# Q projection of layer 0: Strassen's seven products for the last four token tiles, with three tiles in both column halves during the loads

## Chip, cores and metric

The kernel runs on one core of one Trainium2 chip. The metric is the device time of one execution in microseconds (us), the median of several runs. PE is TensorE (matmuls), PEld its weight loads, DVE is VectorE, ACT is ScalarE, POOL is GpSimd and SP is SyncE, which here only issues DMAs.

## What is computed

The program is two layers on 1024 tokens (4 images of 16 x 16) with 1024 channels, all in float32. Layer 0 is the part that the change touches:

```python
x = x + L0(_gn(x))                         # group norm over 32 groups
q = _bn(einsum('bhwc,cd->bhwd', x, Wq))    # 1024 x 1024 times 1024 x 1024
k = softmax(einsum('bhwc,cd->bhwd', x, Wk))  # 256 columns
v = _bn(einsum('bhwc,cd->bhwd', x, Wv))      # 256 columns
# then a content part k.v.q and a part over relative positions, both linear in q
```

Layer 1 is causal attention with 16 heads and a mixture of 8 experts. It follows layer 0 and is the larger part of the time.

## The kernel before

**Q of layer 0.** The normalised input lies in `xn` as 8 chunks of 128 channels by 1024 tokens, the weight in two tiles `w_q[0]` and `w_q[1]`, one for each half (512) of its columns. The output has 8 token tiles `t` times 2 column halves `kc`, 16 products of 128 x 512. Each is a sum over the 8 chunks, so 128 matmuls (`q_product`, L294-295).

**Early products.** The input comes in chunk by chunk (L214-216: `xn` and `w_q[0]` of a chunk; `w_q[1]` as one load behind them, L217). While chunks arrive, six products grow together, tiles 0 to 5 of column half 0, in six PSUM banks (`early`, L310). Between their matmuls lie the group norm of the next chunk: `group_means`, `group_spreads`, `group_norm`, on DVE, ACT and PE. This loop is in an order written by hand (`manual_schedule`, L316). At its end DVE takes the reciprocal of `var_q` and makes scale and shift of the batch norm (L337, `batch_norms`).

**The other products.** The ten remaining products then run one after the other, each in a bank of the ring `mm` (3 banks; a second ring is `tr`, also 3). Outside of the hand-written stretches a scheduler sets the order on each engine.

**Leaving PSUM.** `q_out` (L297) takes a product out. One DVE multiplication (L299) by `q_scale` reads PSUM and frees the bank. Four DVE additions of `q_shift` (L303), each 64 partitions x 256 columns, then write the four quarters into `q0`, with a step of 64 bytes between columns. The scaled rows `q_s` have three buffers.

**What follows.** `w_kv` takes the buffer of `w_q[0]` (L348), so its two loads wait for the last use of `w_q[0]`. Eight products `pk` (L357) follow in the `mm` ring; each leaves through a maximum on DVE (`k_top`, L365) and an exponential on ACT (`k_e`, L368), so the fourth `pk` needs the first one's bank back. Then come the position products `pT` (L414), which read `q0` and the windows that POOL copies (L412). POOL also issues the load of `b_proj` (L496) into the buffer of `w_q[1]`.

**Strassen elsewhere.** The v projection of layer 0 and the products of layer 1 already go by seven products in place of eight, with the sums made on DVE (`sums_of_A`, L149).

Of the kernel before, what the change touches and what calls it, by code (L numbers as in the profile page):

```python
# [32 lines left out]
F32 = mybir.dt.float32  # L33
# [6 lines left out]
P = 128  # L40
C = 1024
NC = C // P
# [3 lines left out]
NT = TOK // P  # L46
# [9 lines left out]
HALF = 512  # L56
# [11 lines left out]
def kernel(  # L68
# [27 lines left out]
    nc = tc.nc  # L96

    def pool(stack, name, bufs=1, **kw):
        return stack.enter_context(tc.tile_pool(name=name, bufs=bufs, reuse_waits="tile", **kw))
# [10 lines left out]
    def big_tile(n, name, shape=(NC, TOK)):  # L110
        return big[n].tile([P, *shape], F32, tag="big", name=name)

    def w_tile(name, *parts, home=None, queue=nc.sync):

        w = (home or wpool).tile([P, NC, HALF], F32, tag="w", name=name)
        at = 0
        for part in parts:
            n = part.shape[1]
            queue.dma_start(w[:, :, at : at + n], part.rearrange("(c p) n -> p c n", p=P))
            at += n  # L120
        return w

    def mm(name):
        return ps.tile([P, HALF], F32, tag="mm", name=name)

    def tr(name):
        return ps.tile([P, HALF], F32, tag="tr", name=name)
# [82 lines left out]
    with ExitStack() as layer0:  # L210
        l0 = pool(layer0, "l0")
        xn = x_pool.tile([P, NC, TOK], F32, tag="x", name="xn")
        w_q = [wpool.tile([P, NC, HALF], F32, tag="w", name=f"w_q{kc}") for kc in range(2)]
        for c in range(NC):  # L214
            nc.sync.dma_start(xn[:, c, :], xT[ts(c, P), :])
            nc.sync.dma_start(w_q[0][:, c, :], Wq[ts(c, P), :HALF])
        nc.sync.dma_start(w_q[1], Wq[:, HALF:].rearrange("(c p) n -> p c n", p=P))  # L217

        vp = l0.tile([P, 4, 2], F32, tag="vp", name="vp")
        for i, a in enumerate((v_gamma, v_beta, v_mean, v_var)):  # L220
# [6 lines left out]
        with ExitStack() as projection:  # L227
            proj, projw = pool(projection, "proj"), pool(projection, "projw", 2)
# [17 lines left out]
            def group_means(c):  # L246
                stats = small.tile([P, B, 6], F32, tag="gn_stats", name=f"gn_stats{c}")
                mv = small.tile([P, B, 2], F32, tag="gn_mv", name=f"gn_mv{c}")
                for b in range(B):
                    nc.vector.bn_stats(stats[:, b, :], xn[:, c, ts(b, M)])  # L250
                    nc.vector.bn_aggr(mv[:, b, :], stats[:, b, :])
                pm = tr(f"gn_pm{c}")
                nc.tensor.matmul(pm[:, :B], average, mv[:, :, 0], start=True, stop=True)
                chunks[c] = mv, pm

            def group_spreads(c):
                mv, pm = chunks[c]
                mean = small.tile([P, B], F32, tag="gn_mean", name=f"gn_mean{c}")
                nc.vector.tensor_copy(mean, pm[:, :B])
                spread = small.tile([P, B], F32, tag="gn_spread", name=f"gn_spread{c}")  # L260
                nc.vector.tensor_sub(spread, mv[:, :, 0], mean)
                nc.vector.tensor_mul(spread, spread, spread)
                nc.vector.tensor_add(spread, spread, mv[:, :, 1])
                pv = tr(f"gn_pv{c}")
                nc.tensor.matmul(pv[:, :B], average, spread, start=True, stop=True)
                chunks[c] = mean, pv

            def group_norm(c):
                mean, pv = chunks[c]
                rstd = small.tile([P, B], F32, tag="gn_rstd", name=f"gn_rstd{c}")  # L270
                inverse_root(rstd, pv[:, :B], EPS)
                less = small.tile([P, B], F32, tag="gn_less", name=f"gn_less{c}")
                nc.vector.scalar_tensor_tensor(less, mean, -1.0, rstd, ALU.mult, ALU.mult)
                for b in range(B):
                    nc.scalar.activation(
                        xn[:, c, ts(b, M)],
                        xn[:, c, ts(b, M)],
                        AF.Identity,
                        bias=less[:, b : b + 1],
                        scale=rstd[:, b : b + 1],  # L280
                    )
# [12 lines left out]
            def q_product(pq, kc, t, c):  # L294
                nc.tensor.matmul(pq, xn[:, c, ts(t, P)], w_q[kc][:, c, :], start=(c == 0), stop=(c == NC - 1))  # L295

            def q_out(pq, kc, t):  # L297
                q_s = projw.tile([P, HALF], F32, tag="q_s", name=f"q_s{kc}_{t}", bufs=3)
                nc.vector.tensor_mul(q_s, pq, q_scale[:, ts(kc, HALF)])  # L299
                for hl in range(2):  # L300
                    rows = slice(hl * 64, hl * 64 + 64)
                    for kl in range(2):
                        nc.vector.tensor_add(  # L303
                            q0[kl * 64 : kl * 64 + 64, kc, :, :, 2 * t + hl].rearrange("p i j -> p (i j)"),
                            q_s[rows, ts(kl, M)],
                            q_shift[rows, kc * HALF + kl * M : kc * HALF + (kl + 1) * M],
                        )

            two = ps.tile([P, 2, HALF], F32, tag="sc", name="pq_two", bufs=1)
            early = [mm(f"pq0_{t}") for t in range(3)] + [two[:, 0, :], two[:, 1, :], tr("pq0_5")]  # L310

            def keep_warm(n):
                for _ in range(n):
                    nc.tensor.matmul(early[0][:, :P], average, average, start=True, stop=True)

            with tc.manual_schedule():  # L316
                keep_warm(14)
                group_means(0)
                keep_warm(3)
                group_spreads(0)  # L320
                keep_warm(5)
                group_norm(0)
                for c in range(NC):
                    for t, pq in enumerate(early):
                        q_product(pq, 0, t, c)
                        if t == 1 and c + 1 < NC:
                            group_means(c + 1)
                        elif t == (3 if c == 0 else 2) and c + 1 < NC:
                            group_spreads(c + 1)
                            group_norm(c + 1)  # L330
                    if c == NC - 4:
                        nc.vector.tensor_scalar(var_q, var_q, BN_EPS, None, ALU.add)
                        nc.scalar.activation(var_q, var_q, AF.Sqrt)
                    elif NC - 4 < c < NC - 1:
                        n = c - (NC - 3)
                        nc.vector.reciprocal(var_q[:, ts(n, M)], var_q[:, ts(n, M)])
                nc.vector.reciprocal(var_q[:, HALF:], var_q[:, HALF:])  # L337
                batch_norms()
            for t, pq in enumerate(early):
                q_out(pq, 0, t)  # L340
            for kc in range(2):
                for t in range(NT):
                    if kc or t >= len(early):
                        pq = mm(f"pq{kc}_{t}")
                        for c in range(NC):
                            q_product(pq, kc, t, c)
                        q_out(pq, kc, t)
            w_kv = w_tile("w_kv", Wk, Wv)  # L348


# [1 line left out]
            for t in range(NT):  # L352
                b, kc = divmod(t, 2)
                pk = mm(f"pk{t}")
                for c in range(NC):
                    for kl in range(2):
# [4 lines left out]
                            start=(c == 0),  # L361
                            stop=(c == NC - 1),
# [33 lines left out]
        for R, first, n_i, T in (  # L396
# [6 lines left out]
            parts = rows * SIDE  # L403
            group = 2 if n_i > S2 else 4
            for n0 in range(0, SIDE, group):
                pT = mm(f"pT{R}_{n0}")
                out_T = pT[:parts, : group * BH * n_i].rearrange("p (j i h) -> p j i h", j=group, h=BH)
                for g in range(group):
# [4 lines left out]
                    for kc in range(2):  # L413
# [4 lines left out]
                            start=(kc == 0),  # L418
                            stop=(kc == 1),
# [3 lines left out]
            for i in range(n_i):  # L423
                ni = first + i
                start = S2 * R + ni - SIDE + 1
# [10 lines left out]
        a11, a12, a21, a22 = (w_kv[:, 4 * j : 4 * j + 4, M + i * P : M + (i + 1) * P] for i in range(2) for j in range(2))  # L436
        b11, b12, b21, b22 = (xn[:, 4 * j : 4 * j + 4, ts(l, HALF)] for j in range(2) for l in range(2))
        c11, c12, c21, c22 = (v_T[:, i, ts(l, HALF)] for i in range(2) for l in range(2))
        s_w = tpool.tile([P, 3, NC // 2, P], F32, tag="s_w", name="s_w", bufs=1)
        s1, s2, s4 = (s_w[:, i, :, :] for i in range(3))  # L440
# [44 lines left out]
        for b, nt in tiles:  # L485
            t = 2 * b + nt
# [10 lines left out]
        with tc.manual_schedule(engines={mybir.EngineType.SP, mybir.EngineType.DVE}):  # L497
            for i, (b, nt) in enumerate(tiles):
# [4 lines left out]
                t = 2 * b + nt  # L503
                for hp in range(2):
                    py = mm(f"py{t}_{hp}")
                    for hl in range(2):
                        bh = b * HEADS0 + 2 * hp + hl
                        for mh in range(2):
# [4 lines left out]
                                start=(mh == 0),  # L513
                                stop=(mh == 1),
# [16 lines left out]
    with ExitStack() as attention:  # L531
# [19 lines left out]
        b11, b12, b21, b22 = (ln1[:, 4 * j : 4 * j + 4, ts(l, HALF)] for j in range(2) for l in range(2))  # L551
# [358 lines left out]
    with ExitStack() as gating:  # L910
# [304 lines left out]
        pairs = ExitStack()  # L1215
        w_odd, two = pool(pairs, "w_odd", 2, side="right"), pool(pairs, "two", 2, side="right")
# [300 lines left out]
```

## Time and profile before

| | |
|---|---|
| median of 3 runs | 1252.16 us (1251.64 to 1252.25) |
| the profiled execution: time, span | 1251.44 us, 1249.6 us |
| granted TensorE clock | 0.998 |
| PE busy | 1231.7 us (99%) |
| DVE busy | 725.6 us (58%) |
| ACT busy | 219.0 us (18%) |
| POOL busy | 359.8 us (29%) |
| DMA moved | 169.21 MB, mean 135 GB/s |
| DMA in the first of 40 slices | 350 GB/s |
| early products and group norm | until 56.4 us of the span |
| the other ten Q products | 57.49 to 126.35 us |
| the eight `pk` products | 126.35 to 154.19 us |

The span goes from the first to the last instruction of the program in one profiled execution; the time of that execution lies 1.8 us above its span. Starts in the timelines are counted from the start of the span. A float32 matmul of the program appears as two matmul records, so that 128 columns by 512 of one chunk are two records.

### The profile page before, as it was taken

How to read it: one execution, taken by the hardware profiler on the slowest of the kernel's cores; microseconds unless marked ns; L12 is line 12 of the kernel's file. 1: busy time of each engine (PE TensorE's matmuls, PEld its weight loads, DVE VectorE, ACT ScalarE, POOL GpSimd, SP SyncE). 2: the span in 40 equal slices, each digit the busy share in tenths (PEclk: the TensorE clock that was granted, in tenths of full speed). 3: DMA queues.
4: the chain of work that ended last, by engine and by line, in shares of the span. 5: the costliest groups of instructions: out<-in, count | busy, mean ns of one | idle time of the engine just before them, and what ended most of it. 6: DMA issues, size and time to landing. Idle time of an engine off the chain costs nothing.

```text
span 1249.6 us, 12749 instructions
## 1 busy us (share of the span) xinstructions
PE 1231.7 (99%) x4556; PEld 643.2 (51%) x4556; DVE 725.6 (58%) x1322; ACT 219.0 (18%) x511; POOL 359.8 (29%) x439
## 2 busy tenths in 40 slices
PE   9999999999999999999999999999999999999998
PEld 5444896777884444444444444444344434434443
DVE  5784325578422566657554866765756646565642
ACT  3300111221000222222221422110110111111110
POOL 0000052241000222232231114445552635363520
PEclk9999999999999999999999999999999999999999
DMA  9020013852202434353383557374856475656442
GB/s 350 18 68 1 17 49 88 320 200 87 68 1 68 124 112 151 118 165 114 102 276 122 187 204 271 71 223 95 245 125 179 105 232 152 153 127 194 100 82 54
DMA packets 91383, 169.21 MB, mean 135 GB/s; under 512 B 9232, under 2 KB 46112, under 8 KB 91312
## 3 DMA queue, kind: packets, MB, share of 16 engines
q1 hardware_dynamic: 73952, 115.83, 27.9%
q0 software_dynamic: 15136, 47.78, 16.0%
q10 hardware_dynamic: 2224, 4.72, 1.1%
q8 instruction: 38, 0.62, 0.2%
q14 instruction: 33, 0.27, 0.1%
HBM read 115.59 MB, written 48.50 MB: 131 GB/s over the span
## 4 chain that ended last, share of the span: by engine, by line
PE 73%; DVE 3%; ACT 1%; issue 1%; DVEq 0%; ACTq 0%
PE p L1284 31%; PE pqk L566 16%; PE po L748 7%; PE pv L566 7%; PE left L1326 3%; PE sc L661 2%; PE pa L730 2%; PE rest L1340 2%; PE last_pe L1442 1%; PE dense_pe L868 1%; PE parts L1006 0%; ACT L132 0%; DVE row_T L177 0%; DVE xb L750 0%; DVE T L1227 0%
## 5 line engine op out<-in xcount | busy, mean ns | idle before, releaser
L853 POOL DMA_INDIRECT w_e_xg<-rows,gather x146 | 155.1, 1062 | 57.3 <-issue 40.2
L1284 PE MATMUL p<-w_e,A 128*128 128x512 f32 x368 | 163.2, 593 | 1.3 <-DVE slot L1119 1.3
L703 POOL TENSOR_TENSOR s_q<-s_q,total 128x128 f32<-128x128 f32 (+1 forms) x128 | 66.2, 547 | 300.3 <-DVE total L700 297.9
L748 PE MATMUL po<-w_p,y_T 128*128 128x512 f32 x256 | 118.5, 605 | 0.0
L1284 PEld LDWEIGHTS p<-w_e,A 128*128 128x128 f32 x368 | 69.6, 190 | 89.9 <-issue 89.2
L1284 PE MATMUL p<-T,S 128*128 128x512 f32 x256 | 112.8, 593 | 0.0
L876 POOL DMA_INDIRECT out_dram<-y,add x32 | 57.0, 1781 | 176.5 <-ACT y L1290 120.2
L1290 ACT ACTIVATE y<-y,slot 128x512 f32<-128x512 f32 x64 | 46.1, 721 | 335.0 <-DVE y L1298 177.1
L295 PE MATMUL pq<-w_q,xn 128*128 128x512 f32 x224 | 99.6, 596 | 1.4 <-DVE q_s L299 1.1
L689 ACT ACTIVATE s_q<-s,top 128x256 f32<-128x256 f32 (+1 forms) x128 | 56.6, 443 | 186.1 <-issue 146.7
L566 PE MATMUL pqk<-ln,w_qk 128*128 128x512 f32 x192 | 85.6, 595 | 0.0
L1284 PEld LDWEIGHTS p<-T,S 128*128 128x128 f32 x256 | 48.5, 190 | 61.1 <-issue 60.3
L748 PEld LDWEIGHTS po<-w_p,y_T 128*128 128x128 f32 x256 | 45.9, 190 | 47.9 <-issue 46.9
L177 DVE STREAM_TRANSPOSE A<-w_e_xg 128x1024 f32<-128x1024 f32 x32 | 39.6, 1239 | 49.9 <-DMA w_e_xg<-rows,gather 49.8
L295 PEld LDWEIGHTS pq<-w_q,xn 128*128 128x128 f32 x224 | 41.8, 190 | 51.8 <-issue 47.4
L566 PE MATMUL pqk<-T,S_qk 128*128 128x512 f32 x128 | 58.5, 600 | 0.0
L566 PEld LDWEIGHTS pqk<-ln,w_qk 128*128 128x128 f32 x192 | 36.0, 190 | 43.3 <-issue 42.3
L1284 PE MATMUL p<-T,A 128*128 128x512 f32 x128 | 57.5, 592 | 0.0
L1284 PE MATMUL p<-w_e,S 128*128 128x512 f32 x128 | 57.5, 592 | 0.0
L566 PE MATMUL pv<-w_v,ln 128*128 128x256 f32 x192 | 44.3, 381 | 1.4 <-DVE ln L177 0.9
L1326 PE MATMUL left<-w_e,one 128*32 128x512 f32 x312 | 41.8, 593 | 0.0
L414 PE MATMUL pT<-q,window 128*128 128x256 f32 (+3 forms) x256 | 40.4, 320 | 0.0
(296 smaller groups left out, 1760.9 us busy)
## 6 DMA issues: line engine op xcount, KB each, us to landing
w_e<-in_expert_w_dram SPq DMA_DIRECT2D x14, 2048.0 KB, 12.9
s_rows<-s_q SPq DMA_DIRECT2D x32, 384.0 KB, 2.6
s_rows<-s_rows SPq DMA_DIRECT2D x128, 96.0 KB, 2.3
w_qk<-in_W_attnT_dram SPq DMA_DIRECT2D x8, 1024.0 KB, 6.0
xn<-in_xT_dram SPq DMA_DIRECT2D x8, 512.0 KB, 8.0
x_at<-in_x_dram SPq DMA_DIRECT2D x8, 512.0 KB, 7.6
w_v<-in_W_attnT_dram SPq DMA_DIRECT2D x2, 2048.0 KB, 12.4
x_rows<-x_at POOLq DMA_DIRECT2D x8, 512.0 KB, 3.9
```

Of the source, the lines that this page charges most:

```text
L177: nc.vector.transpose(row_T[:, :, :slots].rearrange("p c (g j) -> p g c j", j=32), row[:, : slots // 32, :].rearrange("p g (c i) -> p g c ...
L295: nc.tensor.matmul(pq, xn[:, c, ts(t, P)], w_q[kc][:, c, :], start=(c == 0), stop=(c == NC - 1))
L414: nc.tensor.matmul(out_T[:, g, :, :], window[:, kc, :, :].rearrange("p i j -> p (i j)"), q0[:, kc, first : first + n_i, nj, :], start=(kc ...
L566: nc.tensor.matmul(bank, stationary(c), moving(c), start=(c == 0), stop=(c == NC // 2 - 1))
L689: nc.scalar.activation(blocks(h, qt), s[:, h, cols].rearrange("p (b f i) -> p b f i", f=Q, i=32), AF.Exp, bias=top[:, qt, h : h + 1], accu ...
L703: nc.gpsimd.tensor_mul(blocks(h, qt), blocks(h, qt), total[:, qt, h : h + 1].unsqueeze(2).unsqueeze(3).to_broadcast([P, 1 + qt, Q, 32]),)
L748: nc.tensor.matmul(po, y_T[:, c, ts(t, P)], w_p[j][:, c, :], start=(c == 0), stop=(c == NC - 1))
L853: nc.gpsimd.indirect_dma_start(out=row[:, g, :], out_offset=None, in_=table[: (TOK - P) * Q, :] if e in SHORT else table, in_offset=bass.I ...
L876: nc.gpsimd.indirect_dma_start(out=out[: TOK - P, :] if e in SHORT else out, out_offset=bass.IndirectOffsetOnAxis(ap=add[:slots, e, k : k ...
L1284: nc.tensor.matmul(bank, a[:, c, :], b[:, c, :], start=(c == 0), stop=(c == NC // 2 - 1))
L1290: nc.scalar.mul(y[i][:, ts(j, HALF)], y[i][:, ts(j, HALF)], slot[:, e, 1, 2 * pair + i : 2 * pair + i + 1])
L1326: nc.tensor.matmul(bank[ts(i, 32), :], stationary, w[of][j][:, c, :], start=(c == 0), stop=(c == NC - 1))
```

## The change

The loads of `w_q[1]` now come chunk by chunk beside those of `w_q[0]`. The six early products are tiles 0 to 2 of both column halves, in place of tiles 0 to 5 of half 0. Tile 3 follows plainly in both halves. Tiles 4 and 5 form one pair, tiles 6 and 7 another: each pair is a 2 x 2 block product (two token tiles by two halves of the channels, times two halves of the channels by two column halves), done in seven products of 4 matmuls each. The sums of the left side go to `q_parts`, a tile in a buffer that was free at this time; those of the right side are made in place in `w_q`, once for both pairs. The results are added up in `q_parts` and scaled there in place. Of the four additions of each `q_out`, the two that stay on their partitions now run on POOL.

```diff
-            nc.sync.dma_start(w_q[0][:, c, :], Wq[ts(c, P), :HALF])
-        nc.sync.dma_start(w_q[1], Wq[:, HALF:].rearrange("(c p) n -> p c n", p=P))
+            for kc in range(2):
+                nc.sync.dma_start(w_q[kc][:, c, :], Wq[ts(c, P), ts(kc, HALF)])
...
-            def q_out(pq, kc, t):
-                q_s = projw.tile([P, HALF], F32, tag="q_s", name=f"q_s{kc}_{t}", bufs=3)
+            def q_out(pq, kc, t, q_s=None):
+                if q_s is None:
+                    q_s = projw.tile([P, HALF], F32, tag="q_s", name=f"q_s{kc}_{t}", bufs=3)
                 nc.vector.tensor_mul(q_s, pq, q_scale[:, ts(kc, HALF)])
                 for hl in range(2):
                     rows = slice(hl * 64, hl * 64 + 64)
                     for kl in range(2):
-                        nc.vector.tensor_add(
+                        (nc.gpsimd if kl == hl else nc.vector).tensor_add(
...
-            early = [mm(f"pq0_{t}") for t in range(3)] + [two[:, 0, :], two[:, 1, :], tr("pq0_5")]
+            early = [mm(f"pq0_{t}") for t in range(3)] + [two[:, 0, :], two[:, 1, :], tr("pq1_2")]
...
-                        q_product(pq, 0, t, c)
+                        q_product(pq, t // 3, t % 3, c)
...
+            parts = big_tile(0, "q_parts").rearrange("p a b -> p (a b)")
+            b11, b12, b21, b22 = (w_q[l][:, 4 * j : 4 * j + 4, :] for j in range(2) for l in range(2))
+            pairs = []
+            for pair in range(2):
+                a = [xn[:, 4 * j : 4 * j + 4, ts(4 + 2 * pair + i, P)] for i in range(2) for j in range(2)]
+                homes = [parts[:, ts(8 * pair + i, HALF)] for i in range(8)]
...
+                nc.vector.tensor_add(s1, a[2], a[3])
+                nc.vector.tensor_sub(s2, s1, a[0])
+                nc.vector.tensor_sub(s4, a[1], s2)
+                nc.vector.tensor_sub(s3, a[2], a[0])
+            for n in (1, 2, 3, 5, 4, 7, 6):
+                for pair, ((a11, a12, a21, a22), (c11, c12, c21, c22), (s1, s2, s3, s4)) in enumerate(pairs):
+                    a, b = {
+                        1: (a11, b11),
+                        2: (a12, b21),
+                        3: (s4, b22),
+                        5: (s1, b11),
+                        4: (a22, b21),
+                        7: (s3, b12),
+                        6: (s2, b22),
+                    }[n]
+                    bank = (mm if n % 2 else tr)(f"pq_pair{pair}_{n}")
+                    for c in range(NC // 2):
+                        nc.tensor.matmul(bank, a[:, c, :], b[:, c, :], start=(c == 0), stop=(c == NC // 2 - 1))
+                    if n == 1:
+                        nc.scalar.copy(c22, bank)
+                        nc.scalar.copy(c21, bank)
+                    elif n == 2:
+                        nc.vector.tensor_add(c11, bank, c22)
+                        q_out(c11, 0, 4 + 2 * pair, c11)
+                    elif n == 3:
+                        nc.vector.tensor_add(c12, bank, c22)
+                    for to in {5: (c12, c22), 4: (c21,), 7: (c21, c22), 6: (c12, c21, c22)}.get(n, ()):
+                        nc.vector.tensor_add(to, bank, to)
+                    if n == 6:
+                        q_out(c12, 1, 4 + 2 * pair, c12)
+                        q_out(c21, 0, 5 + 2 * pair, c21)
+                        q_out(c22, 1, 5 + 2 * pair, c22)
+                if n == 1:
+                    nc.vector.tensor_sub(b11, b12, b11)
+                    nc.vector.tensor_sub(b12, b12, b22)
+                elif n == 3:
+                    nc.vector.tensor_sub(b22, b22, b11)
+                    nc.vector.tensor_sub(b21, b21, b22)
```

In the built program the order of instructions differs from before only up to the softmax of `pk`; behind it both programs have the same order on every engine.

## The prediction

> **What bounds the kernel now.** First the page, part 1 and the chain of waits by engine.
>
> ```profile
> PE 1231.7 (99%) x4556; PEld 643.2 (51%) x4556; DVE 725.6 (58%) x1322; ACT 219.0 (18%) x511; POOL 359.8 (29%) x439
> ...
> PE 73%; DVE 3%; ACT 1%; issue 1%; DVEq 0%; ACTq 0%
> ```
>
> PE is busy for 99% of the span and makes up the chain, so a matmul less is time less, as long as PE doesn't wait instead. Next the stretches: busy time by engine in the ten plain Q products, then in the `pk` products.
>
> ```profile
> 57.50:126.30 68.80, 68.80 (x160) 30.30 (x160) 45.81 (x80) 1.49 (x2) 0.00 (x0) 1.00 0.10 31
> 126.30:154.20 27.90, 27.90 (x258) 25.52 (x257) 9.66 (x26) 3.96 (x14) 1.97 (x5) 1.00 0.05 19
> ```
>
> After the stretch and its length come PE, PEld, DVE, ACT, POOL. PE has no gap; DVE has 23 us to spare in the first stretch, POOL did nothing. Third, the timeline of PE where the early products end.
>
> ```profile
> 55.34 1.02 PE L295 MATMUL pq<-w_q,xn 128*128 128x512 f32 x2
> 57.49 68.93 PE L295 MATMUL pq<-w_q,xn 128*128 128x512 f32 x160 [1.12 <-DVE q_s L299]
> 126.35 27.91 PE L357 MATMUL pk<-w_kv,xn 128*64 128x256 f32 x256
> ```
>
> Here PE waits 1.12 us for DVE to free the first bank. Last, what POOL and DVE do to each other when both read two SBUF operands, since the change sets 32 POOL additions beside DVE's. Two timelines, of DVE and POOL alone:
>
> ```profile
> 284.34 2.92 POOL L526 TENSOR_TENSOR x_at<-x_at,ln_rows 128x1024 f32<-128x1024 f32 x1 [4.62 <-ACT ln_rows L196]
> 284.97 3.37 DVE L153 TENSOR_TENSOR w_v<-w_v 128x1024 f32<-128x1024 f32 x1
> ...
> 288.26 1.21 DVE L152 TENSOR_TENSOR s_v<-w_v,s_v 128x1024 f32<-128x1024 f32 x1
> ```
>
> ```profile
> 582.65 0.66 DVE L150 TENSOR_TENSOR S_qk<-w_qk 128x512 f32<-128x512 f32 x1
> 582.81 3.60 POOL L703 TENSOR_TENSOR s_q<-s_q,total 128x128 f32<-128x128 f32 x4 [3.38 <-DVE total L700]
> 583.35 0.77 DVE L151 TENSOR_TENSOR S_qk<-S_qk,w_qk 128x512 f32<-128x512 f32 x1
> 584.15 0.98 DVE L152 TENSOR_TENSOR S_qk<-w_qk,S_qk 128x512 f32<-128x512 f32 x1
> 585.06 0.88 DVE L153 TENSOR_TENSOR w_qk<-w_qk 128x512 f32<-128x512 f32 x1
> 585.86 0.68 DVE L650 TENSOR_TENSOR U_qk<-pqk,qk 128x512 f32<-128x512 f32 x1
> ```
>
> The DVE sum beside a POOL addition takes 3.37 us, its like alone 1.21. In the second view four sums start 0.80 us apart where 0.64 is usual (402.37 to 404.30), and the four POOL instructions take 3.60 us where the same four take 1.90 at 531.05. Each side waits for the other in turn.
>
> The Trainium skill (SBUF — State Buffer, Who interferes with whom) has this as a rule: a DVE instruction with two SBUF inputs and a GpSimd instruction that reads SBUF exclude each other for the whole instruction. The first view agrees (3.37 against 1.21 us); the second shows less per instruction.
>
> **Fewer matmuls.** Before, 16 products of 8. After, 8 products of 8 (tiles 0 to 3) and 2 x 7 of 4: 120, not 128. One costs 68.9/80 = 0.861 us, so PE loses 8 x 0.861 = **6.9 us**.
>
> **The 1.12 us gap.** In the built order three matmuls of product 2 (pair 0, in a `tr` bank) stand ahead of tile 3: 2.6 us of work from 56.4 to 58.9. The first `q_s` comes later, as two sums of 0.6 us stand before it on DVE: it ended at 57.43, now at 58.6. The gap goes: **1.1 us**. PE would so reach `pk` at 126.35 - 8.0 = 118.3.
>
> **Loads.** Each chunk now brings 1.05 MB, at 350 GB/s in 3.0 us; PE takes 5.75 us for one (the starts 15.15, 20.89, 26.64). Chunk 0 of `xn` is still first. SP's seven added issues stand ahead of the batch-norm rows and `emb`, with the same bytes before them. Nothing.
>
> **DVE in the chunk loop.** Two sums (1.2 us) move into chunk 4, where DVE waited 1.57 us for PE (29.54). Hidden, with 0.4 us over.
>
> **ACT.** Four copies of 0.59 us, where it idled for 70 us. Hidden.
>
> **w_kv.** Its issue on SP now waits for product 4, which ends 4 x 3.45 = 13.8 us ahead of `pk`; the K part lands 5.5 us after issue (DMA issues). Nothing queues behind it on SP until the position stage. Hidden; without that cover it would cost up to 5.5.
>
> **b_proj.** POOL's issue of it waits for the last product, with eight POOL additions behind it. `pT` needs them, some 30 us later. Hidden.
>
> **q_s.** A scaling on DVE now also waits until POOL has read the buffer three `q_out`s back, with all of DVE's queue behind it. POOL's two additions take some 1.2 us per `q_out` (0.61 for 256 columns, L703), DVE's share 1.8. Hidden, while POOL stays under 0.9 per addition.
>
> **DVE up to the right-hand sums.** From 54.35 to the last addition of tile 3 DVE has, alone: two sums 1.2, three rows of 1024 3.5, eight `q_s` 4.9, sixteen additions 9.6, four sums 2.4, small ones 0.6: until 76.6. The first in-place sum waits for product 1 of both pairs, at 79.6: 3.0 us of slack. Then until product 3 ends (90.7) it has 2 x 2.2 + 5 x 0.61 + 4 x 0.60 = 9.9 us, until 89.6: 1.1 of slack. From there 0.6 + 2 x 2.2 = 5.0 makes b21 ready at 95.8, due for product 4 at 97.6: 1.8. In all 5.9 us of slack for 20 POOL additions.
>
> **DVE's tail: the new wait.** Product 6 of pair 0 ends at 118.3 - 3.45 = 114.9. Before the first `k_top` DVE has six additions from PSUM (0.61), six scalings in place (0.61) and ten column additions (0.60): 13.3 us, until 128.3. `k_top` to the end of `k_e` takes 1.0 (130.13 to 131.15), a hand-over 0.1: the first bank is free at 129.4. The fourth `pk` wants it at 118.3 + 3 x 3.49 = 128.8. So PE waits **0.6 us** even without POOL.
>
> **POOL in the tail.** Ten POOL additions fall into this stretch, each beside a DVE instruction with two SBUF inputs. The price of one is bounded below by 0 (POOL's 2.36 us at 247.42 left the PSUM additions beside it at 0.67), above by 0.54 (the 2.15 us that L153 lost, for a quarter of the columns). In the second view a 256-column POOL instruction cost some 0.4, a 128-column one 0.2. I take 0.30: DVE's column additions hold fewer columns than those sums, so part of POOL's work fits between. Ten cost **3.0 us**. Upstream 20 x 0.30 = 6.0 against 5.9 of slack: nothing. Above that price I count half of what exceeds the slack, since many early additions find DVE waiting or reading PSUM.
>
> **The sum.** -6.9 - 1.1 + 0.6 + 3.0 = -4.4. Behind `pk` both programs have the same order, and PE fills 1177.6 of the 1191.5 us of the stretches tabled from 57.5 on, so it stays: 1251.4 goes to 1247.0 in the profiled execution; that lies 0.7 below the median, which goes to **1247.8 us**. With a price of 0 it is -7.4; with 0.54 it is -8.0 + 0.6 + 5.4 + (10.8 - 5.9)/2 = +0.5.
>
> **Rivals.**
>
> *POOL's additions mostly miss DVE's.* For it: six of the 22 DVE instructions in the tail read PSUM and collide with nothing. Against: the other 16 read SBUF twice, and each pair of POOL additions is released by a scaling right among them. At 0 to 0.15 each the gain is 7.4 to 5.9: 1244.8 to 1246.3.
>
> *The collisions eat the gain.* DVE waits out the whole of POOL's instruction each time, as L153 did. At 0.39 each the tail takes 4.5 and the stretch before it (7.8 - 5.9)/2 = 1.0, which leaves a gain of 2.5, 1249.7; at 0.60 it is 6.6 and 3.0, and 1.6 slower, 1253.8. Against: the mean of the second view.
>
> This is what the Trainium skill's rule of exclusion would give if taken in full: at 0.54, 1252.6 us.
>
> *POOL's strided addition is slow, and the kernel slower.* No POOL instruction of the trace writes columns 64 bytes apart. DVE pays for it: 0.586 us (L303) against 0.42 for 256 plain columns (L600). If POOL needs twice its plain rate, an addition holds 1.08 us in place of 0.54 and the price rises to 0.84: tail 0.6 + 8.4, before it (16.8 - 5.9)/2 = 5.4; 14.4 - 8.0 = 6.4 slower, 1258.6. It decides from a price of 0.64 on: 7.0 + 3.5 = 10.5, that is 2.5 slower. Against: POOL's plain rate, 2.36 us for 1024 columns (L526) or 2.3 ns each, is no faster than DVE's strided one, 0.586 for 256 with its fixed part, so the step may be hidden.
>
> The Trainium skill (GPSIMD Engine Reference, Performance pitfalls for Q7 kernels) puts half as much again on reads with a step over 8 bytes; here the write has the step, and no run here shows POOL's price. With it a collision would cost 0.57, and the time would be about 1253 us, short of the point that decides.
>
> *It doesn't do what it says:* `w_kv` or a chunk late, so that PE waits for a load. The slack is 8 us for the one and 2.7 per chunk for the other.
>
> **Numbers.** Chances: forecast (price 0.15 to 0.39) 0.47, its own range 1246.3 to 1249.7; collisions light 0.23; gain eaten 0.16; strided POOL slow 0.12; a load late 0.02. A measurement of this kernel can tell about 0.2%, 2.5 us. Faster: 0.47 + 0.23 = 0.70; same 0.16; slower 0.14. The range goes from the light end to the end of the eaten case, and leaves out the slow one.
>
> **What would show it.** In the trace after: 240 records of Q products rather than 256; no wait for `q_s` behind the early ones; `pk` without a wait for `w_kv`; a wait of some 3.6 us on the fourth `pk`, released by `k_e`; DVE's additions near 0.9 apart where POOL works. Wrong would be: a POOL addition over 0.9 us when alone, waits on products 4 or 5, or none at the fourth `pk`.

## The result, and the profile after

| | before | after |
|---|---|---|
| median (13 runs each) | 1251.91 us (1251.45 to 1252.43) | 1248.97 us (1248.41 to 1249.39) |
| ratio, with 95% interval | | 0.9977 [0.9968, 0.9985] |
| profiled execution: time, span | 1251.44, 1249.6 us | 1249.13, 1247.3 us |

The change saves 2.9 us, or 0.23%. 1247.8 was forecast. The page of the changed kernel, part 1:

```profile
PE 1227.9 (98%) x4540; PEld 641.3 (51%) x4540; DVE 740.8 (59%) x1322; ACT 221.1 (18%) x515; POOL 390.4 (31%) x471
```

Sixteen PE records are gone (4556 to 4540, two for each of the 8 matmuls), ACT has 4 instructions more and POOL 32, as the diff says. But PE is busy for only 3.8 us less, where eight matmuls are 6.9. Some of the remaining ones must have become longer. The timeline of PE shows where; the first two lines are the early products' end, the others the last Strassen products and `pk`. Columns are start, time, engine, line, operation, then the idle time before it and who ended it.

```profile
55.13 1.02 PE L295 MATMUL pq<-w_q,xn 128*128 128x512 f32 x2
55.99 2.74 PE L376 MATMUL pq_pair<-w_q,xn 128*128 128x512 f32 x6
...
104.31 13.90 PE L376 MATMUL pq_pair<-w_q,q_parts 128*128 128x512 f32 x32
118.14 10.64 PE L407 MATMUL pk<-w_kv,xn 128*64 128x256 f32 x96
132.62 19.17 PE L407 MATMUL pk<-w_kv,xn 128*64 128x256 f32 x160 [3.84 <-ACT k_e L418]
151.71 2.84 PE L496 MATMUL pv<-xn,w_kv 128*128 128x512 f32 x6
```

Before, tile 6 started behind a wait of 1.12 us. Here three matmuls of product 2 stand in that place and nothing waits. `pk` starts at 118.14 rather than 126.35, which is 8.2 us earlier. Then two things give time back. The fourth `pk` waits 3.84 us for the first one's exponential, and the 160 records behind this wait take 19.17 us where the first 96 set a pitch that gives 17.7. So `pv`, the next stage, starts 2.48 us earlier (154.19 before), not 8.2.

The stretch view says why the 160 records are long. After a stretch and its length come busy time (and instructions) of PE, PEld, DVE, ACT and POOL, then the granted TensorE clock (1.00 is full speed), the DMA share and GB/s:

```profile
118.14:151.71 33.57, 29.73 (x257) 25.44 (x256) 21.38 (x40) 3.96 (x14) 11.97 (x17) 0.95 0.04 17
132.60:136.10 3.50, 3.48 (x18) 2.00 (x20) 2.86 (x8) 1.00 (x4) 2.37 (x5) 0.51 0.00 0
136.10:139.60 3.50, 3.50 (x36) 3.19 (x34) 1.37 (x5) 0.70 (x4) 0.00 (x0) 1.00 0.02 5
```

For 3.413 us behind the wait PE runs at half the clock: 18 records in 3.50 us, then 36 in the next 3.50. Half of 3.413 is 1.7 us, lost on top of the wait.

What makes the wait is DVE's tail. Its timeline:

```profile
117.93 3.78 DVE L304 TENSOR_TENSOR q<-q_parts,q_rows 64x256 f32<-64x256 f32 x4
...
123.05 1.57 DVE L304 TENSOR_TENSOR q<-q_parts,q_rows 64x256 f32<-64x256 f32 x2
...
127.15 3.77 DVE L304 TENSOR_TENSOR q<-q_parts,q_rows 64x256 f32<-64x256 f32 x4
130.94 0.69 DVE L300 TENSOR_TENSOR q_parts<-q_parts,q_rows 128x512 f32<-128x512 f32 x1
131.55 0.42 DVE L415 TENSOR_REDUCE k_top<-pk 128x1 f32<-128x256 f32 x1
```

`k_top`, which starts the release of the first `pk` bank, stands behind all of them, though the first `pk` was complete near 121.7 (a third of the 96 records). Four additions beside POOL's take 3.78 us, 0.94 each. The same additions without POOL are in an experiment below.

### The profile page after: what moved, and what is told of

Read it like the earlier page. It is cut to its first block, busy times and chain, and to the rows that moved or that the text cites. A ratio compares the mean times of both kernels' runs of the same rounds, so it can differ in the third digit from the quotient of the medians.

```text
span 1247.3 us, 12776 instructions
## 1 busy us (share of the span) xinstructions
PE 1227.9 (98%) x4540; PEld 641.3 (51%) x4540; DVE 740.8 (59%) x1322; ACT 221.1 (18%) x515; POOL 390.4 (31%) x471
## 4 chain that ended last, share of the span: by engine, by line
PE 74%; DVE 2%; ACT 1%; issue 0%; DVEq 0%; ACTq 0%
PE p L1334 31%; PE pqk L616 16%; PE pv L616 7%; PE po L798 7%; PE left L1376 3%; PE sc L711 2%; PE pa L780 2%; PE rest L1390 2%; PE last_pe L1492 1%; PE dense_pe L918 1%; PE parts L1056 0%; ACT L132 0%; DVE row_T L177 0%; DVE xb L800 0%; DVE T L1277 0%
## 5 line engine op out<-in xcount | busy, mean ns | idle before, releaser
L903 POOL DMA_INDIRECT w_e_xg<-rows,gather x146 | 157.7, 1080 | 57.3 <-issue 40.8
L295 PE MATMUL pq<-w_q,xn 128*128 128x512 f32 x96 | 44.5, 599 | 0.3 <-ACT xn L275 0.3
L616 PEld LDWEIGHTS pv<-w_v,ln 128*128 128x128 f32 x192 | 37.3, 196 | 6.4 <-ACT v L639 1.2
```

What stands on the lines that cost most here:

```text
L616: nc.tensor.matmul(bank, stationary(c), moving(c), start=(c == 0), stop=(c == NC // 2 - 1))
L903: nc.gpsimd.indirect_dma_start(out=row[:, g, :], out_offset=None, in_=table[: (TOK - P) * Q, :] if e in SHORT else table, in_offset=bass.I ...
```

## The experiments

Theory: up to `pk` the change gives 8 us, and what is lost is the wait on the fourth `pk`, which DVE's tail and POOL's collisions in it make, together with the half clock that follows the wait. Rivals: the loss lies elsewhere (the loads, POOL's work over all of the stage), or the half clock is chance.

Experiments 1, 3, 4 and 5 ran in one session, in which the kernel before stood at 1253.73 us (9 runs, 1252.59 to 1256.58), 1.8 us above its time in the table and more widely spread. The changed kernel was not run in it. So neither the ratios of these experiments nor their medians beside 1248.97 are good to better than some 2 us, and their traces count for more; experiment 6 compares on one chip.

**1. All additions on DVE.** The changed kernel without POOL's share.

```diff
-                        (nc.gpsimd if kl == hl else nc.vector).tensor_add(
+                        nc.vector.tensor_add(
```

> The changed kernel with all four additions of each q_out on DVE, as before the change. Theory (moving two of four to POOL shortens DVE's queue by more than the collisions give back): the tail has ten more additions of 0.6 us in place of ten collisions of 0.34, so the fourth pk waits 3.84 + 2.6 = 6.4 us; ahead of product 4 there are 20 x 0.6 = 12 us more against 5.9 us of slack, 6 us of waits; with one or two half clocks 1256 to 1260 us, slower than before. Rival (the collisions cost as much as the move saves): about 1249.

Measured: 1259.49 us (1257.56 to 1260.29), ratio 1.0041 [1.0028, 1.0055]: slower than before. Timeline of PE:

```profile
77.69 7.99 PE L376 MATMUL pq_pair<-w_q,xn 128*128 128x512 f32 x18 [2.02 <-DVE q_s L300]
...
102.98 8.83 PE L376 MATMUL pq_pair<-w_q,xn 128*128 128x512 f32 x16 [3.57 <-DVE w_q L397]
...
136.04 2.84 PE L496 MATMUL pv<-xn,w_kv 128*128 128x512 f32 x6
142.48 13.84 PE L407 MATMUL pk<-w_kv,xn 128*64 128x256 f32 x100 [3.59 <-ACT k_e L418]
```

DVE alone is too slow: PE waits for a scaled row, for the right-hand sum b21 (L397), and at the fourth `pk` for 6.4 us, of which 2.84 are filled by matmuls of `pv`, which the scheduler put there in this version. Half clock follows the second and the third wait, for one and for two windows:

```profile
103.86:107.26 3.40, 3.40 (x5) 1.35 (x4) 1.46 (x3) 0.00 (x0) 0.00 (x0) 0.50 0.00 0
141.40:148.22 6.82, 5.74 (x28) 3.24 (x30) 4.88 (x14) 1.70 (x6) 0.00 (x0) 0.50 0.00 0
```

POOL's share, with all its collisions, is what makes the seven products pay.

**2. The loads alone, and POOL's share alone.** The kernel before with chunk-wise `w_q[1]` and three tiles in both halves, and the kernel before with two of four additions on POOL; no Strassen in either.

```diff
-            nc.sync.dma_start(w_q[0][:, c, :], Wq[ts(c, P), :HALF])
-        nc.sync.dma_start(w_q[1], Wq[:, HALF:].rearrange("(c p) n -> p c n", p=P))
+            for kc in range(2):
+                nc.sync.dma_start(w_q[kc][:, c, :], Wq[ts(c, P), ts(kc, HALF)])
...
-                        q_product(pq, 0, t, c)
+                        q_product(pq, t // 3, t % 3, c)
...
```

The edit for POOL's share is the line with `nc.gpsimd` in the change.

> The kernel before with only the loads of the change (w_q of both halves by chunk) and its six early products (tiles 0 to 2 in both halves); the ten others run plainly, without Strassen, all additions on DVE. Theory (loads and early products are hidden and worth nothing by themselves): the same chunk pitch of 5.75 us, the 1.1 us wait for the first q_s stays, 1251.9 us within 0.5. Rival (the larger chunks arrive late, or the var_q rows do): waits in the chunk loop, up to 3 us slower.

> The kernel before with only the move of two of the four additions of each q_out to POOL. Theory (DVE is not what PE waits for in the plain Q stage): no change, 1251.9 us within 0.5; DVE's column additions 0.6 us where POOL is done, 0.9 where it works. Rival (the share on POOL is a gain or a loss by itself): 1 us or more either way.

Measured, beside 1252.57 us (21 runs) of before: 1251.27 us (1250.70 to 1252.33), ratio 0.9989 [0.9980, 0.9998] for the loads; 1252.43 us (1251.94 to 1252.81), ratio 0.9997 [0.9988, 1.0006] for POOL's share. Neither moves the time by more than 0.2%. Each lies at most 0.2 us outside its expected band, which was set from the 1251.9 of before; here before stood 0.7 higher. Both keep the wait for the first `q_s`; here in the timeline of the loads alone:

```profile
57.14 3.27 PE L295 MATMUL pq<-w_q,xn 128*128 128x512 f32 x7 [1.13 <-DVE q_s L299]
...
126.00 27.91 PE L357 MATMUL pk<-w_kv,xn 128*64 128x256 f32 x256
```

The 0.35 us by which `pk` starts earlier than before are there at the last early product (54.99 against 55.34). So the loads are hidden, and the 1.1 us come from the matmuls of product 2 that stand in the gap, not from the other order of tiles. Before Strassen DVE had room, so that POOL's help is worth nothing there and its collisions cost nothing.

**3. POOL's tail additions later.** The twelve POOL additions of the last three `q_out` of both pairs are held until the third softmax step. DVE's order stays.

```diff
+                        if kl == hl and hold:
+                            held.append(operands)
+                        else:
+                            (nc.gpsimd if kl == hl else nc.vector).tensor_add(*operands)
...
+                if t == 2:
+                    gate = small.tile([P, 1], F32, tag="gate", name="gate", bufs=1)
+                    opened = nc.gpsimd.tensor_copy(gate, total)
+                    with tc.issue_after(opened.ins):
+                        for operands in held:
+                            nc.gpsimd.tensor_add(*operands)
```

> The changed kernel with POOL's twelve additions of the last six q_outs held back, by a small copy on POOL that reads a result of the third softmax step; DVE's order is unchanged. Theory (DVE's tail is longer by 3.0 to 3.4 us because POOL's additions shut it out of SBUF, ten times 0.3): DVE's column additions in the tail are 0.6 us apart, the fourth pk waits 0.6 us, no half clock; 1249.0 - 3.2 - 1.7 = 1244.1 us. Rival (DVE's column additions are slow by themselves, or the queue is simply too long): they stay near 0.94 us apart, the wait stays near 3.8 us, 1249.0.

Measured: 1245.59 us (1245.40 to 1246.99), ratio 0.9937 [0.9924, 0.9951]. The timelines of DVE, PE and POOL:

```profile
117.67 2.38 DVE L314 TENSOR_TENSOR q<-q_parts,q_rows 64x256 f32<-64x256 f32 x4
...
128.14 0.42 DVE L421 TENSOR_REDUCE k_top<-pk 128x1 f32<-128x256 f32 x1
```

```profile
129.21 17.55 PE L413 MATMUL pk<-w_kv,xn 128*64 128x256 f32 x160 [0.69 <-ACT k_e L424]
```

```profile
132.79 9.60 POOL L432 TENSOR_TENSOR q<-q_parts,q_rows 64x256 f32<-64x256 f32 x12
```

Without POOL the four additions take 2.38 us, 0.60 each, in place of 0.94. From the start of `pk` to the first `k_top` it is 128.14 - 117.88 = 10.26 us; with POOL it is 131.55 - 118.14 = 13.41. The ten POOL additions thus cost DVE 3.15 us, **0.31 each**. The wait falls to 0.69 us, no half clock follows it, and the 160 records take 17.55 us. POOL's strided addition takes 0.80 us here. `pv` starts 5.0 us earlier than in the changed kernel (146.69 against 151.71), near the 4.9 expected (3.2 + 1.7). The median misses its forecast of 1244.1 by 1.5 us: the session may account for some of it, and the profiled execution has a half clock from 277.48 on, behind another wait.

**4. The wait kept, PE busy in it.** Twelve matmuls of 128 x 128 that nothing reads stand ahead of the fourth `pk`.

```diff
+                if t == 3:
+                    fill = tr("fill")
+                    for _ in range(12):
+                        nc.tensor.matmul(fill[:, :P], average, average, start=True, stop=True)
                 pk = mm(f"pk{t}")
```

> The changed kernel with twelve matmuls of 128 x 128 that nobody reads, in a free bank, ahead of the fourth pk: 3.3 us of work inside its wait of 3.8. Theory (the half clock of 3.4 us after that wait comes from the wait): the clock stays at 1.0 in the pk stretch, the fourth pk starts at the same time, and 1.7 us go: 1247.3 us. Rival (the half clock has another cause): it stays, 1249.0; if the filler takes longer than the wait, above that.

Measured: 1247.61 us (1246.72 to 1249.75), ratio 0.9951 [0.9937, 0.9964]. Timeline of PE:

```profile
128.57 2.94 PE L407 MATMUL fill<-average 128*128 128x128 f32 x24
132.50 17.55 PE L411 MATMUL pk<-w_kv,xn 128*64 128x256 f32 x160 [0.99 <-ACT k_e L422]
149.98 2.84 PE L500 MATMUL pv<-xn,w_kv 128*128 128x512 f32 x6
```

The stretch behind the wait, which was at 0.51 in the changed kernel:

```profile
132.60:136.10 3.50, 3.50 (x34) 3.24 (x36) 2.75 (x8) 1.11 (x4) 2.26 (x5) 1.00 0.03 5
```

The fourth `pk` starts as late as in the changed kernel (132.50 against 132.62), since DVE is no faster. Yet `pv` starts 1.73 us earlier (149.98 against 151.71): useless work in the wait keeps the clock whole. This separates the two parts of the loss, 3.84 us of waiting and 1.7 us of half clock. The median is 1.4 us under the changed kernel's, but from another session. The profiled execution itself, 1249.75 us, is the slowest of the five: 3.3 us of its lead over the kernel before go between 760 and 909 us, far behind the change, with one half-clock window from 769.69 on; what took the rest is open.

**5. The last four `q_out` later.** DVE issues each of them behind the softmax step of one of the first four `pk`, so that `k_top` no longer stands behind them.

```diff
-                        q_out(c12, 1, 4 + 2 * pair, c12)
-                        q_out(c21, 0, 5 + 2 * pair, c21)
-                        q_out(c22, 1, 5 + 2 * pair, c22)
+                        late += [(c12, 1, 4 + 2 * pair), (c21, 0, 5 + 2 * pair), (c22, 1, 5 + 2 * pair)]
+                        while pair == 0 and len(late) > 1:
+                            of, kc, t = late.pop(0)
+                            q_out(of, kc, t, of)
...
-                nc.vector.tensor_scalar(k_q[:, b, kc, :], k_e, total, None, ALU.mult)
+                k_done = nc.vector.tensor_scalar(k_q[:, b, kc, :], k_e, total, None, ALU.mult)
+                if late:
+                    of, to_kc, to_t = late.pop(0)
+                    with tc.issue_after(k_done.ins):
+                        q_out(of, to_kc, to_t, of)
```

> The changed kernel with its last four q_outs (of the two pairs) issued one by one behind the softmax steps of the first four pk, so that DVE's maximum of the first pk is not behind them. Theory (PE's wait on the fourth pk comes from DVE's queue in front of the first k_top, and the half clock behind it from that wait): no wait at the fourth pk, granted clock 1.0 in the whole pk stretch, 3.8 + 1.7 = 5.5 us less than the changed kernel, 1243.5 us. Rival (the bank comes late for another reason, such as the load of w_kv or the exponential): the wait stays near 3.8 us and the time at 1249.0.

Measured: 1244.48 us (1242.77 to 1244.93), 1.0 above the forecast, ratio 0.9922 [0.9908, 0.9936]. Timeline of PE:

```profile
118.44 27.91 PE L408 MATMUL pk<-w_kv,xn 128*64 128x256 f32 x256
146.28 2.84 PE L501 MATMUL pv<-xn,w_kv 128*128 128x512 f32 x6
```

All 256 records run through in 27.91 us, as before the change, and `pv` starts 7.91 us earlier. POOL's and DVE's additions still collide here; what is late no longer matters, since `q0` is complete by 139 and first read by `pT` behind `pv`.

**6. Both once more on one chip.** The changed kernel and the version of experiment 5, unchanged, side by side, for a direct comparison and for profiles in which the clock's windows lie otherwise.

> The changed kernel once more, unchanged, for a second profile with other edges of the 3.413 us windows. If a window in which PE idles for half its length or more is followed by one at half clock, the 3.84 us wait at the fourth pk brings one at any offset (at least 1.9 us of it fall into one window), so pv starts about 2.5 us earlier than before, not 4.2; the 1.85 us wait near 279 us brings one only if nearly all of it falls into one window. Time 1248.4 to 1249.4. If the half clock of the first profile was chance, no 0.5 follows the wait here, and pv starts 4.2 us earlier, time near 1247.2.

> The last four q_out behind the softmax steps, beside the changed kernel on the same chip. If the wait at the fourth pk and its half clock are all that was lost, this is 4 to 5 us under the changed kernel: 1243.5 to 1245 against 1248.4 to 1249.4. If the gain of the first run came from its chip, the two are within 2 us.

Measured: the changed kernel 1249.09 us (11 runs, 1248.57 to 1249.78), ratio to before (1251.64, 15 runs) 0.9980 [0.9971, 0.9989]; the later `q_out` 1243.38 us (1242.39 to 1244.02), ratio 0.9935 [0.9921, 0.9948], 0.1 us under its expected band. On the same chip the rearranged version is 5.7 us faster than the changed kernel and 8.3 us faster than the one before: it is the best of all. Stretches of the changed kernel's second profile:

```profile
128.39:132.25 3.86, 0.00 (x1) 0.00 (x0) 3.79 (x6) 0.56 (x2) 2.52 (x4) 0.91 0.00 0
132.30:138.30 6.00, 6.00 (x29) 3.30 (x31) 3.31 (x10) 1.13 (x4) 2.31 (x5) 0.50 0.00 0
138.40:141.80 3.40, 3.40 (x36) 3.08 (x34) 0.94 (x3) 0.57 (x2) 0.00 (x0) 1.00 0.03 5
```

The same wait, 3.86 us, and again half clock behind it, this time for two windows: the clock goes down at 131.56, inside the wait, and up 6.83 us later. So it is no chance, but its length depends on where the windows lie: the wait now costs 3.9 and about 2.9 more (the 160 records take 20.50 us), and `pv` starts 1.5 us earlier than before, not the 2.5 expected (0.57 us of the 1.5 were there at the last early product, 54.77 against 55.34). In the first of the two windows PE still idled for 0.69 us (131.56 to 132.25), and in the first of the two of experiment 1 for 1.08 (141.40 to 142.48). The other seven falls to half clock in the ten profiles, the one at each program's end left out, lasted one window, and PE worked throughout that window.

## Why the prediction was right, and where its sum was off

The direction and the mechanism were right: matmuls gone, then a new wait of DVE's making at the fourth `pk`. The gain of 4.4 us in the profiled execution came out as 2.3 (1251.44 to 1249.13), and the medians differ by 2.9. The median of 1248.97 lies in the forecast's own range, 1246.3 to 1249.7, though a cost of more than 2 us in the profile was not in the sum: the range was made for the price of a collision and had room for it, which is luck.

- **Fewer matmuls and the gap: -8.0 forecast, -8.21 measured** at the start of `pk`, of which 0.21 were there at the last early product (55.13 against 55.34). No wait for `q_s` behind the early products; three matmuls of product 2 lie there, as worked out.
- **Loads, ACT, `w_kv`, `b_proj`, the `q_s` ring: nothing, as forecast.** No wait of PE names a load or one of ACT's copies, DVE has no wait for POOL in this stage, and the loads alone leave the time within 0.2%.
- **Slack up to the right-hand sums: held, by a hair.** 6.0 us of collisions were set against 5.9 of slack. That it held by so little is in part luck. The last sum, in DVE's timeline of the changed kernel, ends at 97.28:

```profile
94.99 2.29 DVE L397 TENSOR_TENSOR w_q<-w_q,w_q 128x2048 f32<-128x2048 f32 x1
97.20 2.48 DVE L386 TENSOR_TENSOR q_parts<-pq_pair,q_parts 128x512 f32<-128x512 f32 x4
```

  Product 4 starts at 97.34. Any more work on DVE becomes a wait of PE, as the first experiment shows with 3.57 us.
- **The tail: 3.6 us of wait forecast, 3.84 measured.** A collision was priced at 0.30, a choice between 0 and 0.54 from instructions of other shapes, and costs 0.31 (3.15 us for ten); that it is so close is luck, that it is well under 0.54 is not; the tail alone was put at 10.0 us from the start of `pk` and is 10.26.
- **The step that was missing is the clock.** The sum took the work behind the wait at its old duration ("so it stays"). The prediction forecast a wait of 3.6 us and put down 3.6; its real price was 3.84 + 1.7. The Trainium skill (TensorE: Matmul & The Clock Gate, What's actually happening) describes such a gate: windows of about 3.4 us that run on by themselves, and half the clock after an idle one. The trace agrees on the length, 3.413 us, and on the half, and differs on how much idle time it takes (below); the two falls to half clock of the first profile lie 150.186 us apart, 44 windows. It was not weighed in the prediction. Taken at its word, an idle window, it would have given the missing 1.7 in the first profile, where PE worked for 0.01 us of the window ahead of the fall (129.22 to 132.63), but not in the second, where PE worked for 0.25 us of it (128.14 to 131.56) and the clock fell all the same.
- **A second half clock, further on, was also not forecast.** Both kernels have a wait of 1.85 us for a layer norm's rows near 280 us (L200 waits for L196). In the first profile of the changed kernel half clock follows it:

```profile
279.40:282.81 3.41, 1.62 (x11) 1.34 (x12) 2.91 (x5) 2.78 (x6) 0.94 (x1) 1.00 0.00 0
282.82:286.22 3.40, 3.40 (x10) 2.69 (x9) 3.40 (x2) 0.30 (x1) 2.53 (x2) 0.50 0.11 10
```

  It takes 0.57 us from the gain (the lead over before falls from 2.48 to 1.91): the 40 records behind it take about 1.4 us longer, and a wait of 0.86 us for DVE among them, which the kernel before has, is gone.

The profiled sum: from the start of `pk` to that of `pv` it takes 33.57 us, where before it took 27.84 (126.35 to 154.19). These 5.73 are 3.84 of idle time, 1.7 of half clock and 0.2 that neither row shows. -8.21 + 5.73 + 0.57 = -1.91, and PE's last matmul ends 2.03 us earlier.

**The rivals.** *Light collisions* falls with 0.31 a piece. *The gain eaten* needed 0.39 and more; no DVE addition waited out a whole POOL instruction of 0.80 to 0.88 us. One POOL and one DVE addition take 0.94 us together, where one behind the other they would take 0.80 + 0.60 = 1.40, so they overlap in part. The Trainium skill (SBUF — State Buffer, Who interferes with whom), read as one whole exclusion for each POOL addition, would ask for 0.80 us a piece, an estimate at POOL's measured duration; the experiment without POOL in the tail shows 0.31. *Strided POOL slow* falls too: 0.80 us, where 0.9 was the limit named and 1.08 the rival's figure. It is slower than the 0.61 taken for plain columns, though.

What stays open is when exactly a wait brings half clock. With the grid of 3.413 us laid from the first rise of the clock, PE's idle time in the fullest window around that 1.85 us wait was 1.79, 1.90 and 1.90 us in three profiles with half clock behind it, and 1.29 to 1.62 us in six without. That would be a limit of about half a window, but in the second profile of the later `q_out` 1.85 us of idle time was followed by a full clock:

```profile
272.03:275.44 3.41, 1.56 (x9) 1.06 (x8) 1.53 (x4) 1.64 (x4) 0.00 (x0) 1.00 0.25 100
275.44:278.85 3.41, 3.36 (x20) 2.84 (x19) 3.41 (x2) 1.53 (x3) 2.92 (x1) 1.00 0.00 0
```

And near 770 and 780 us two profiles with 1.56 and 1.57 us show half clock. So idle time alone does not decide it for waits of this length. The four windows with more (2.51 and 2.54 us in experiment 1, 3.16 and 3.40 at the fourth `pk`) all brought it. The first wait of experiment 1, 2.02 us long, did not: an edge of the grid divides it into 0.87 and 1.14.

## What to carry to other kernels

When matmuls leave the path, look for what the next bank release stands behind on its engine: here additions that nobody needed soon held a 0.4 us maximum back by eight microseconds (13.41 us behind the start of `pk` against 5.40 with the later `q_out`), and moving them gave 5.7 us where the change alone gave 2.6. Price a new wait of PE with the half clock behind it (1.7 us for each window of 3.4): it always came here when 2.5 us or more of the wait fell into one window, and at times from 1.6 on. Useless matmuls in the wait avoided that part. Additions shared between DVE and POOL are worth having where DVE is the limit even at 0.3 us of collision each, and worth nothing where it isn't.

## What the runs showed of the hardware

- In all ten profiles the granted clock changes only on a grid of 3.413 us, and one wait of 3.84 or 3.86 us cost one half-clock window in one profile, two in another (1.7 or about 2.9 us with the idle part taken off), of the same kernel.
- A wait well short of a window, 1.85 us, can bring half clock: it did in three of ten profiles.
- POOL writes 64 x 256 float32 with a step of 64 bytes in 0.80 us without DVE's additions beside it, and in 0.88 with them; a DVE addition of that shape goes from 0.60 to 0.94 us when four of each run together, and to 0.78 for two.
